# A perceiver block on one core: the first rooms of the way up, the transposes ahead of it, and two operations of its last units are placed differently

## The chip, the cores and the metric

The kernel runs on one core of a Trainium2 chip. The metric is the time of one execution on the device in microseconds (us). Times of single instructions come from one execution recorded by the hardware profiler.

The core has a matrix engine, TensorE (PE in the profile; its weight loads are PEld), and VectorE (DVE), ScalarE (ACT) and GpSimd (POOL) for work on tiles. SyncE (SP) issues most of the transfers; SPq, ACTq and POOLq are the queues for them. Matmul results go to banks of the accumulator memory (PSUM), from where DVE and ACT take them.

## The reference

There are 32 sequences of 64 tokens with 512 features. Three stages each add to x:

```
x = x + xattn(layernorm(x), ctx, mask)          # attention over 256 context rows
x = x + attn(layernorm(x), wq, wkv, wo, ...)    # 16 heads, causal, low rank
x = x + ffn(layernorm(x), gate, up, down, expert, gamma, beta)

def ffn(t):
    logits = t @ gate                            # 8 gates
    scale  = sum of the two largest logits
    h = square(relu(t @ up))                     # 512 -> 2048
    y = h @ down + (t @ expert) * scale          # 2048 -> 512
    return layernorm(y) * gamma + beta
```

## The kernel before, in words

Every float32 operand is split into a high part, which ACT copies (`split`, L147), and a low part, the rest, which DVE subtracts (L149). A product is then three matmuls: high by high, low by high, high by low (`mm3`, L174 on). The large products are tiled 2 by 2 and each tile of the four needs seven products instead of eight (`SEVEN`); GpSimd makes the sums that this needs (`sums`, L155), and `combine` (L158 to L169) puts the seven results together: a copy by ACT (L160), then DVE's L162, L163, L165, L166 and L168. Each of these frees a bank that PE wants for the unit after next.

The stages by time in the profile: projections and the context attention to about 240 us, the attention to about 550, **the way out** (product with wo, L718 to L726) to about 758, **the way up** (L1144 on) from 773 to 931, **the way down** from 931 to 1086, then the last layer norm.

The way out goes through units (block of 256 tokens, slot k of 8). Beside its units the code places other work by unit number: `TURN_AT` transposes a finished block (`o_t`), `MULT_AT` multiplies it by the expert (`o_expert`), `UP_READ` and `UP_PUT` read slots of the up weights and split them (`put_slot`, four instructions: two copies on ACT, two subtractions on DVE). After the last unit come the transposes of the last block (L985 on), three of the four parts of its split features (`right`, xr0_0 to xr0_2; copies at L1067, subtractions at L1065), and the last `o_expert` (cpe14, cpe15, L179 to L181), whose output tile `mo` is stored by ACT's queue (L1023). Then the way up begins.

The way up has four passes (b = 0 to 3) of eight units (n = 0 to 7, slots in the order 0, 1, 5, 6, 7, 2, 3, 4). A unit is 42 matmuls of 256 columns (`up_seven`, L1156), its four banks come from one of two pools in turn (`ps_f[n % 2]`), its combination ends in a tile `uo`, ACT applies relu and square (L1226, L1227), and the result goes to memory as `hd`. In a pass the next pass's features are split (xr1_0 to xr1_3, and so on). In the first pass the remaining up slots are split, one in each unit; in the last pass the down slots are split (`put_slot(..., "down")`) and the first pairs of the way down are read back and split (`read_home`, L698; `left`, which gives the tiles `hl`). `read_home` reads into a tile that is there from the start; `left(u, pins=...)` is the split of unit u.

`settle(n, ...)` issues n transposes of a 128 by 128 tile into a bank whose content isn't used. It stands ahead of the way up (n = 8) and at units 5 and 32 of the way down (n = 4).

The order on each engine is made by the framework's scheduler out of the order of the program, its own cost estimates, and the tiles' rooms: a new tile in a room waits for the last reader of the old one. `with after(ins)` (the `pins` of `split`, `right`, `put_slot` and `left`) sets an operation no earlier in the order than `ins`; without it the scheduler may place the operation as far ahead as its inputs allow. Each engine then works its list in that order.

Two rooms matter for the change: `mo0` is allocated ahead of the way out (L1070), and the last `o_expert` uses a later tile of the same pool, `ap`; that pool closes ahead of the way up, and the tiles of the pool `fp` (`uo`, `up1`) take over its space.

Of the kernel before, what the change touches and what calls it, by code (L numbers as in the profile page):

```python
# [18 lines left out]
P = 128  # L19
# [36 lines left out]
MULT_AT = (21, 25, 31, 39, 47, 55, 63)  # L56

FEATURES_AT = (2, 4)
UP_READ, UP_PUT = (1, 2, 5, 6, 7), (3, 5)

BETA_AT = 60

# [24 lines left out]
def perceiver_block(ctx: ExitStack, tc: tile.TileContext, x, mem, mask, wq_a, bq_a, qnw, wq_b, bq_b,  # L87
# [87 lines left out]
    def mm3(ps, pairs):  # L175

        n = len(pairs)
        for j, (ah, al, bh, bl) in enumerate(pairs):
            nc.tensor.matmul(ps, ah, bh, start=(j == 0), stop=False)  # L179
            nc.tensor.matmul(ps, al, bh, start=False, stop=False)  # L180
            nc.tensor.matmul(ps, ah, bl, start=False, stop=(j == n - 1))  # L181


    with ExitStack() as mla:
# [816 lines left out]

    def o_expert(blk, xh, xl, _):

        mo = mos.pop(blk, None) or ap.tile([P, 2, D], FP, tag="mo", name=f"mo{blk}")
        for tt in range(2):
            i = 2 * blk + tt
            sl = slice(tt * P, (tt + 1) * P)
            pes = []
            for c in (slice(256, NE), slice(0, 256)):
                pe = ps_t.tile([P, D], FP, tag="T", name=f"cpe{i}_{c.start}")  # L1010
                mm3(pe[:, 0 : c.stop - c.start], [
                    (xh[:, k, sl], xl[:, k, sl], wes[0][:, k, c], wes[1][:, k, c]) for k in range(NKD)
                ])
                pes.append(pe)
            t8 = sp.tile([P, 8], FP, tag="t8", name=f"t8{i}")
            nc.vector.max(t8, pes[0][:, 256:264])
            gs = sp.tile([P, 1], FP, tag="gs", name=f"gs{i}")
            nc.vector.tensor_tensor(gs, t8[:, 0:1], t8[:, 1:2], ALU.add)
            if tt:
                yield  # L1020
            nc.scalar.mul(mo[:, tt, 256:512], pes[0][:, 0:256], gs)
            nc.scalar.mul(mo[:, tt, 0:256], pes[1][:, 0:256], gs)
        nc.scalar.dma_start(mo_d[blk], mo)  # L1023
        yield

    xr, xc, xw = {}, {}, []

    def read_x(b, kk, room=None, behind=None):

# [37 lines left out]
                    ins = nc.scalar.copy(t[:, to], src)  # L1067
        return ins

    mos = {0: ap.tile([P, 2, D], FP, tag="mo", name="mo0")}  # L1070
    put_slot(ORDER[2], "wo")
    xt, xns, xT, x2s, dones, read = {}, {}, {}, {}, {}, 5
    for u, (blk, k) in enumerate(out_units):
# [61 lines left out]
    xT = o_t(NB - 1, xns.pop(NB - 1), lambda: next(scaled))  # L1135
    for part in range(3):
        right(0, part, (dones[NB - 1][0], xT[2][1]))
    put_slot(ORDER[2], "up", pins=xT[2])
    for _ in o_expert(NB - 1, *xT):
        pass  # L1140
    pc.close()


# [2 lines left out]
    with ExitStack() as pu:  # L1146
# [3 lines left out]
        def up_seven(ps, k, b, n, steps):  # L1150
            wh, wl = (t[:, 0:7].rearrange("p a (k f) -> p a k f", k=2) for t in wts[k])

            def product(s, parts, first=False, last=False):
                i, j = SEVEN[s]
                for m, (kk, w, low) in enumerate(parts):
                    nc.tensor.matmul(  # L1156
                        ps[s // 2][:, s % 2], w[:, i, kk], xr[b, 2 * kk + low][:, j],
                        start=(first and m == 0), stop=(last and m == len(parts) - 1),
                    )

            most = [(0, wh, 0), (0, wl, 0), (0, wh, 1), (1, wh, 0), (1, wl, 0)]
            rest = [(1, wh, 1)]
            one, two = (0, 2, 4, 6), (1, 3, 5)
            late = None
            if n == 0:
                with after(settle(8, ps, wh[:, 0, 0], ident2, None) if b == 0 else None):
                    for s in one:
                        product(s, most, first=True)
            if n == 7:
                for s in one:  # L1170
                    product(s, rest, first=True)
                for s in (0, 2, 4):
                    product(s, most, last=True)
                for s in two:
                    product(s, rest, first=True)
                if b + 1 < NB // 2:
                    late = right(b + 1, 3)
            for s in range(7):
                if n == 0 and s in one:
                    product(s, rest, last=True)  # L1180
                elif n < 7:
                    product(s, most + rest, True, True)
                elif s in two or s == 6:
                    product(s, most, last=True)
                if s in (1, 3, 5, 6):
                    with after(late if s == 3 else None):
                        next(steps)
# [8 lines left out]
                nc.sync.dma_start(h_d[b][:, k, 3:7], w)  # L1196

        stores = []
        right(0, 3)
        behind = read_slot(ORDER[5], "up", behind=reads[-1])  # L1200
        for b in range(NB // 2):
            if b == NB // 2 - 1:
                first = [(blk, k) for ks in (ORDER[:5], ORDER[5:]) for blk in DOWN[:2] for k in ks]
                out_units[:] = first + [(blk, k) for blk in DOWN[2:] for k in ORDER]
            for n, k in enumerate(ORDER):
                m = n - 3 if b == 0 else n - 1
                summed = None
                if 0 < b < NB // 2 - 1 and m in (0, 1):
                    read_x(b + 1, m)
                if b == 0 and n in (1, 2):  # L1210
                    behind = read_x(1, n - 1, x_room(1, n - 1), behind)
                if b == 0 and n in (0, 1):
                    behind = read_slot(ORDER[n + 6], "up", behind=behind)
                if b == NB // 2 - 1 and 0 < n < 7:
                    read_slot(ORDER[n - 1], "down")
                if b == NB // 2 - 1 and n == 4:
                    read_home(2, from_h, None)
                if b == NB // 2 - 1 and n in (5, 6):
                    read_pair(n - 2, from_h)
                ps = banks(ps_f[n % 2], f"up{b}_{k}")  # L1220
                o = fp.tile([P, 5, TB], FP, tag="o", name=f"uo{b}_{k}")
                p1 = fp.tile([P, TB], FP, tag="p1", bufs=2, name=f"up1_{b}_{k}")
                done = []
                up_seven(ps, k, b, n, combine(p1, ps, o, done))
                for q in (slice(0, 2), slice(2, 4)):
                    nc.scalar.activation(o[:, q], o[:, q], AF.Relu)  # L1226
                    act = nc.scalar.activation(o[:, q], o[:, q], AF.Square)  # L1227
                pins = (act, done[-1])
                o4 = o[:, 0:4].rearrange("p (c t) (a n) -> p c t a n", c=2, a=2)
                w = None  # L1230
                if not bare(b, k):
                    w = ccp.tile([P, 8, P], FP, tag="c", name=f"uw{b}_{k}").rearrange("p (d t) n -> p d t n", t=2)
                    at = [o4[:, i, :, a] for i in range(2) for a in range(2)] + [w[:, d] for d in range(4)]
                    summed = sums(at, LEFT)
                if b == 0 and n < 5:
                    put_slot(ORDER[n + 3], "up", pins=pins)
                if b == NB // 2 - 1 and 1 < n < 7:
                    put_slot(ORDER[n - 2], "down", pins=pins)
                if b == NB // 2 - 1 and n == 2:
                    for u in range(2):  # L1240
                        read_home(u, from_h, None)
                if b == NB // 2 - 1 and n == 3:
                    left(0, pins=(done[0], done[-1]))
                if b == NB // 2 - 1 and n == 5:
                    left(1, pins=(done[0], done[-1]))
                if b == NB // 2 - 1 and n == 6:
                    left(2, pins=(done[0], done[-1]))
                if b == NB // 2 - 1 and n == 7:
                    read_pair(5, from_h)
                if stores and (b, n) != (NB // 2 - 1, 7):  # L1250
                    store_h(*stores.pop(0))
                stores.append((b, k, o4, w))
                if b + 1 < NB // 2:
                    if m in (0, 1):
                        sum_x(b + 1, m, summed)
                    for q in (PARTS_FIRST if b == 0 else PARTS).get(m, ()):
                        right(b + 1, q, pins)

    with ExitStack() as pd:
# [82 lines left out]
        for u, (blk, k) in enumerate(out_units):  # L1342
            if k == ORDER[0]:
                pss[blk] = banks(ps_f[DOWN.index(blk) % 2], f"dp{blk}")
            while read <= min(max(u + READ_AHEAD, 2 * u + 1), u + READ_FAR, last_unit):
                read_pair(read, from_h, room_for(read))
                read += 1
            for v in [v for v in bares if v <= u + SUM_AHEAD]:
                c = bares.pop(v)
                with after(pows[-1]):  # L1350
# [15 lines left out]
                store_h(*stores.pop(0))  # L1366
            if u == 6:
                nc.sync.dma_start(gab, gamma.partition_broadcast(P))
            if u in (4, 6, 8):
                put_slot(ORDER[3 + u // 2], "down")  # L1370
            if u in (2, 4):
                read_slot(ORDER[5 + u // 2], "down")
            outs = [d for d in outs if step(d, low)]
# [52 lines left out]
```

## Time and profile before

| what | before |
|---|---|
| median of three timed runs | 1103.37 us (1101.33 to 1103.40) |
| the profiled execution | 1098.9 us |
| its span | 1096.7 us |
| its granted TensorE clock, mean | 0.998 |
| PE busy | 97% of the span |
| DVE, ACT, POOL busy | 70%, 50%, 46% |
| matmuls | 10201 |
| PE waits: op L725 for DVE hl L149 | 3.7 us in 4 |
| PE waits: ops L985 for DVE on L139 | 1.0 us in 1 |
| PE waits: up L1156 for DVE uo L168 | 0.6 us in 1 |

How to read it: a line of a view names an engine, a line of the code, the operation and its tiles, out<-in. The timeline's rows start with the start and the duration in us; in brackets stands the idle time of the engine just before, and after "<-" what ended it. Matmuls are pipelined: a record lasts about 0.28 us while the next one starts after about 0.115, so rows overlap. A row of the view by stretch gives, for each engine, the time that it was busy and in brackets its instructions, then the granted clock, the share of the DMA engines and GB/s.

### The profile page before, as it was taken

The page shows a single profiled execution, that of the slowest core. Times are in us where ns is not written, and L with a number is a line of the kernel's source. Part 1 is how long each engine was busy: PE and PEld are TensorE (multiplying, and loading weights), DVE is VectorE, ACT ScalarE, POOL GpSimd, SP SyncE. Part 2 cuts the span into 40 slices and gives each one's busy share as a digit, 9 for nine tenths or more (in the row PEclk, how much of TensorE's full clock was granted, in tenths as well). Part 3 has the DMA queues.
Part 4 walks back from the last instruction along what each step waited for, and adds up shares of the span by engine and source line. Part 5 has one row for each costly group of instructions (what it writes and reads, how often), then busy time and mean ns, then how long its engine had stood idle before and what let it go on. Part 6 is the DMA issues. An engine that isn't in the chain of part 4 may idle for free.

```text
span 1096.7 us, 26072 instructions
## 1 busy us (share of the span) xinstructions
PE 1066.9 (97%) x10201; PEld 983.6 (90%) x10201; DVE 769.0 (70%) x1369; ACT 546.1 (50%) x1051; POOL 508.1 (46%) x691
## 2 busy tenths in 40 slices
PE   8999999999999999999998999999999999999996
PEld 6667777679999999999988999999999999999996
DVE  5666666657666666656787866667785658898786
ACT  4444444533433444434475544445676567755553
POOL 2333333326788778874570000003238970065671
PEclk9999999999999999999999999999999999999999
DMA  8867666343776778655487776779646689998672
GB/s 259 263 216 231 206 212 203 124 161 121 260 234 245 260 247 294 249 207 195 160 324 276 263 241 213 231 235 359 218 156 202 221 247 366 310 309 257 206 232 79
DMA packets 195386, 254.67 MB, mean 232 GB/s; under 512 B 18544, under 2 KB 140032, under 8 KB 195264
## 3 DMA queue, kind: packets, MB, share of 16 engines
q1 hardware_dynamic: 190704, 240.92, 67.0%
q10 hardware_dynamic: 3456, 8.39, 2.2%
q0 software_dynamic: 1104, 3.70, 0.9%
q8 instruction: 80, 1.31, 0.5%
q14 instruction: 42, 0.34, 0.1%
HBM read 146.67 MB, written 106.30 MB: 231 GB/s over the span
## 4 chain that ended last, share of the span: by engine, by line
PE 59%; DMA 10%; POOL 9%; DVE 8%; issue 7%; ACT 5%; SPq 1%; DVEq 0%; POOLq 0%; ACTq 0%
PE up L1156 9%; PE pss L773 5%; PE psq L179 4%; PE psq L180 4%; PE psq L181 4%; PE op L725 3%; PE op L726 3%; PE op L723 3%; PE psv L817 3%; DMA hd<-uo 2%; PE pse L179 2%; PE pse L181 2%; PE pse L180 2%; DMA x1d<-xt 2%; DMA vd<-vw 2%
## 5 line engine op out<-in xcount | busy, mean ns | idle before, releaser
L755 DVE SCALAR_TENSOR_TENSOR qe<-pse,bqp,cq 64x256 f32<-64x256 f32 x256 | 123.7, 483 | 76.5 <-PE pse L181 70.7
L1156 PE MATMUL up<-xr,wh_up 128*128 128x256 f32 x896 | 157.6, 280 | 0.6 <-DVE uo L168 0.6
L1156 PEld LDWEIGHTS up<-xr,wh_up 128*128 128x128 f32 x896 | 137.5, 189 | 1.0 <-issue 0.7
L725 PE MATMUL op<-wh_wo,hl 128*128 128x256 f32 x448 | 124.4, 279 | 3.7 <-DVE hl L149 3.7
L723 PE MATMUL op<-wh_wo,hl 128*128 128x256 f32 x448 | 124.0, 280 | 0.6 <-ACT hl L147 0.6
L725 PE MATMUL dp<-wh_down,hl 128*128 128x256 f32 x448 | 124.5, 278 | 0.0
L723 PE MATMUL dp<-wh_down,hl 128*128 128x256 f32 x448 | 124.4, 278 | 0.0
L726 PE MATMUL dp<-wl_down,hl 128*128 128x256 f32 x448 | 124.3, 277 | 0.0
L149 DVE TENSOR_TENSOR hl<-c,hl 128x896 fp32r<-128x896 f32 x84 | 94.3, 1126 | 42.3 <-ACT hl L147 42.0
L1156 PE MATMUL up<-xr,wl_up 128*128 128x256 f32 x448 | 123.7, 280 | 0.0
L726 PE MATMUL op<-wl_wo,hl 128*128 128x256 f32 x448 | 123.5, 277 | 0.0
L147 ACT CAST hl<-c 128x896 fp32r<-128x896 f32 x84 | 79.0, 942 | 77.7 <-PE op L726 38.0
L179 PE MATMUL psq<-qa_hi,qh 128*128 128x256 f32 x384 | 112.5, 293 | 0.0
L180 PE MATMUL psq<-qa_hi,ql 128*128 128x256 f32 x384 | 106.4, 277 | 0.0
L181 PE MATMUL psq<-qa_lo,qh 128*128 128x256 f32 x384 | 106.2, 276 | 0.0
L725 PEld LDWEIGHTS op<-wh_wo,hl 128*128 128x128 f32 x448 | 84.3, 188 | 4.8 <-DVE hl L149 4.7
L723 PEld LDWEIGHTS op<-wh_wo,hl 128*128 128x128 f32 x448 | 83.6, 188 | 1.5 <-ACT hl L147 0.8
L723 PEld LDWEIGHTS dp<-wh_down,hl 128*128 128x128 f32 x448 | 84.6, 189 | 0.0
L725 PEld LDWEIGHTS dp<-wh_down,hl 128*128 128x128 f32 x448 | 84.1, 188 | 0.4 <-DVE hl L149 0.4
L1156 PEld LDWEIGHTS up<-xr,wl_up 128*128 128x128 f32 x448 | 84.2, 188 | 0.0
L726 PEld LDWEIGHTS op<-wl_wo,hl 128*128 128x128 f32 x448 | 84.1, 188 | 0.0
L726 PEld LDWEIGHTS dp<-wl_down,hl 128*128 128x128 f32 x448 | 84.1, 188 | 0.0
(233 smaller groups left out, 3146.6 us busy)
## 6 DMA issues: line engine op xcount, KB each, us to landing
c<-vd SPq DMA_DIRECT2D x58, 448.0 KB, 4.2
cx<-in_ctx SPq DMA_DIRECT2D x32, 512.0 KB, 4.6
vd<-vw SPq DMA_DIRECT2D x29, 512.0 KB, 3.6
hd<-uo SPq DMA_DIRECT2D x107, 128.0 KB, 3.3
hd<-uw SPq DMA_DIRECT2D x21, 512.0 KB, 3.3
dcw<-hd SPq DMA_DIRECT2D x18, 448.0 KB, 5.6
vd<-v SPq DMA_DIRECT2D x30, 256.0 KB, 3.5
wd_wo<-pw_wo SPq DMA_DIRECT2D x8, 896.0 KB, 4.9
```

The costliest lines, as they stand in the source:

```text
L147: copy = nc.scalar.copy(hi, src)
L149: return copy, engine.tensor_tensor(lo, src, hi.bitcast(FP), ALU.subtract)
L179: nc.tensor.matmul(ps, ah, bh, start=(j == 0), stop=False)
L180: nc.tensor.matmul(ps, al, bh, start=False, stop=False)
L181: nc.tensor.matmul(ps, ah, bl, start=False, stop=(j == n - 1))
L723: first = nc.tensor.matmul(ps[s // 2][:, s % 2], h[:, a], wh[:, b], start=(k == 0 and s % 2 == 0), stop=False)
L725: nc.tensor.matmul(ps[s // 2][:, s % 2], l[:, a], wh[:, b], start=False, stop=False)
L726: ins = nc.tensor.matmul(ps[s // 2][:, s % 2], h[:, a], wl[:, b], start=False, stop=last)
L755: rope = nc.vector.scalar_tensor_tensor(qe[64 * a : 64 * a + 64, :], pe[r, :], bqp[r, p : p + 1], cq[r, a, :], ALU.add, ALU.mult,)
L773: nc.tensor.matmul(ps[64 * j : 64 * j + 64, pj, b, :], qs[2 * pj + j][a][:, sl], kT[:, a, kt], start=(a == 0), stop=(a == 1),)
L817: nc.tensor.matmul(o, kv[a, i, :], t[a, bp, :], start=True, stop=True)
L1156: nc.tensor.matmul(ps[s // 2][:, s % 2], w[:, i, kk], xr[b, 2 * kk + low][:, j], start=(first and m == 0), stop=(last and m == len(parts) ...
```

## The change

It has four parts. First, `UP_PUT` loses its second unit: the up slot `ORDER[1]` is no longer split at the fifth unit of the last block but just ahead of the last `o_expert`, pinned behind the last unit's split and the low part of the last transposes. The slot `ORDER[2]`, which stood there, goes to the start of the way up, its low part pinned behind `right(0, 3)`. Second, `mo0` is no longer allocated ahead; each `o_expert` takes its own tile. So the first rooms of the way up lie elsewhere. Third, `mm3` returns its last matmul, and the settling transposes ahead of the way up become four, pinned behind the last one of the expert. Fourth, in the last pass the slot `ORDER[4]` for the way down and the split `left(2)` leave unit 6: the slot goes to unit 1 and `left(2)` to unit 0 of the way down's loop, both without pins.

```diff
-UP_READ, UP_PUT = (1, 2, 5, 6, 7), (3, 5)
+UP_READ, UP_PUT = (1, 2, 5, 6, 7), (3,)
...
-            nc.tensor.matmul(ps, ah, bl, start=False, stop=(j == n - 1))
+            ins = nc.tensor.matmul(ps, ah, bl, start=False, stop=(j == n - 1))
+        return ins
...
-        mo = mos.pop(blk, None) or ap.tile([P, 2, D], FP, tag="mo", name=f"mo{blk}")
+        mo = ap.tile([P, 2, D], FP, tag="mo", name=f"mo{blk}")
...
-                mm3(pe[:, 0 : c.stop - c.start], [
+                made.append(mm3(pe[:, 0 : c.stop - c.start], [
                     (xh[:, k, sl], xl[:, k, sl], wes[0][:, k, c], wes[1][:, k, c]) for k in range(NKD)
-                ])
+                ]))
...
-    mos = {0: ap.tile([P, 2, D], FP, tag="mo", name="mo0")}
     put_slot(ORDER[2], "wo")
...
-    put_slot(ORDER[2], "up", pins=xT[2])
+    put_slot(ORDER[1], "up", pins=(low[0], xT[2][1]))
     for _ in o_expert(NB - 1, *xT):
         pass
+    ends = made[-1]
...
-                with after(settle(8, ps, wh[:, 0, 0], ident2, None) if b == 0 else None):
+                with after(settle(4, ps, wh[:, 0, 0], ident2, ends) if b == 0 else None):
...
-        right(0, 3)
+        put_slot(ORDER[2], "up", pins=(xT[2][0], right(0, 3)))
...
-                if b == NB // 2 - 1 and 1 < n < 7:
+                if b == NB // 2 - 1 and 1 < n < 6:
                     put_slot(ORDER[n - 2], "down", pins=pins)
...
-                if b == NB // 2 - 1 and n == 6:
-                    left(2, pins=(done[0], done[-1]))
...
+            if u == 0:
+                left(2)
...
-            if u in (4, 6, 8):
-                put_slot(ORDER[3 + u // 2], "down")
+            if u in (1, 4, 6, 8):
+                put_slot(ORDER[max(4, 3 + u // 2)], "down")
```

In the order of the instructions that results, up to 755 us nothing is moved. From there: the settling transposes stand four together ahead of the way up, where before one stood there and seven among the matmuls of the last expert; in the first pass, L168 of each combination stands ahead of the splits, where it stood behind them; the two low halves of xr1_3 stand ahead of the combination of `uo0_3`, where they stood behind it; the ACT copy of `left(2)` stands ahead of the relu of `uo3_0`, where it stood behind the copy L160 of `up1_3_3`; and half of a `wl_down` split stands between L162 and L163 of `uo3_3`. The order on SP and on POOL's queue is nearly the same.

More of the change, by code (lines that the diff above doesn't have):

```diff
@@ L1024, in o_expert @@
         yield
-    xr, xc, xw = {}, {}, []
+    xr, xc, xw, made = {}, {}, [], []
     def read_x(b, kk, room=None, behind=None):
```

## The prediction

> **What bounds the kernel now.** I read the busy shares first, then the waits, then counts of matmuls by stretch, then the rows of the three small engines around the places that the change touches.
>
> ```profile
> span 1096.7 us, 26072 instructions
> PE 1066.9 (97%) x10201; PEld 983.6 (90%) x10201; DVE 769.0 (70%) x1369; ACT 546.1 (50%) x1051; POOL 508.1 (46%) x691
> L1156 PE MATMUL up<-xr,wh_up 128*128 128x256 f32 x896 | 157.6, 280 | 0.6 <-DVE uo L168 0.6
> ```
>
> TensorE (PE) is busy for 97% of the span. The group of the way up (L1156) shows 0.6 us of idle time in 896 matmuls. So two things alone can move the end: a pause of PE, and the spacing of its matmuls. The change removes no matmul; work that it moves on VectorE (DVE), ScalarE (ACT) or a queue counts only through PE's pauses.
>
> The spacing isn't one number. In the view of busy time by stretch, the third value is PE's time and the (x) its matmuls:
>
> ```profile
> 773.00:793.00 20.00, 20.00 (x172) 20.00 (x171) 14.02 (x23) 11.88 (x23) 5.83 (x8) 1.00 0.54 183
> 810.00:830.00 20.00, 20.00 (x179) 20.00 (x178) 13.40 (x25) 12.99 (x26) 16.37 (x21) 1.00 0.71 233
> 860.00:880.00 20.00, 20.00 (x172) 20.00 (x171) 12.09 (x21) 10.96 (x20) 18.12 (x23) 1.00 0.66 220
> 950.00:970.00 20.00, 20.00 (x179) 20.00 (x178) 15.31 (x17) 11.07 (x16) 10.33 (x14) 1.00 1.14 316
> ```
>
> All four are full of matmuls of one shape, PE is never idle, the granted clock is 1.00, and yet 172 or 179 matmuls fit. A record lasts 0.28 us and both ends count, so the spacing is 20.28/172 = 117.9 ns or 20.28/179 = 113.3 ns: 4.5 ns, or 4%, apart. Followed along the trace, the spacing keeps its value for long stretches and changes after a pause (fast after the one at 808.0, slow again after two of 0.1 us at 847), or at the four "settle" transposes in the way down (slow to fast at 943.5 and 1065.5, two of two). The way up begins slow at 773.07, is fast for 330 of its 1344 matmuls (809 to 847), and slow for the other 1014.
>
> **The change, part by part.** The sum is made against the profiled execution's 1098.9 us (span 1096.7 and 2.2 around it), 4.5 below the median of 1103.4; the difference found is then put on the median.
>
> *1. Settling transposes.* Before, one of the eight stands directly ahead of the way up, and seven lie among the last expert's matmuls. After, all four that are left stand together behind the last of them. Four in a row take 943.41 to 944.09, 0.67 us, where two matmuls take 0.24: 0.44 for four, 0.11 for one. **+0.33 us.** What it buys is term 6.
>
> *2. Handover from the way out.* One slot's split leaves unit 61, where DVE holds it ahead of the last combination:
>
> ```profile
> 755.37 2.63 DVE L149 TENSOR_TENSOR wl_up<-wl_up,wh_up 128x1024 fp32r<-128x1024 f32 x2
> 757.92 0.68 DVE L162 TENSOR_TENSOR oo<-op,op 128x512 f32<-128x512 f32 x1
> 764.13 1.00 DVE L139 TENSOR_SCALAR on<-oo,lnmv_o,rs_o 128x512 f32<-128x512 f32 x2 [0.74 <-POOL rs_o L127]
> ```
>
> L162 could start at 757.05, when the products of its bank are done, 0.87 earlier. The MAX8 of the expert (L1016) then stands ready no sooner than 759.55, which eats part: the chain to L139 and the transposes comes 0.65 us earlier. PE idles 1.02 us there ("PE ops L985 <- DVE on L139"), so all of it is gained. **−0.65**, between 0 and −1.02. The split itself (2.6 us of DVE, 1.8 of ACT) moves to 769–776 beside the last expert and the first up unit, where DVE next idles 4.67 us (to 780.10); the first rooms no longer wait for the store of the expert's output, so that the first combination starts some 2.7 us earlier and the extra split fits.
>
> *3. The stall at 808.*
>
> ```profile
> 803.28 0.68 DVE L166 TENSOR_TENSOR uo<-up,up 128x512 f32<-128x512 f32 x1
> 804.29 2.10 DVE L149 TENSOR_TENSOR wl_up<-wl_up,wh_up 128x1024 fp32r<-128x1024 f32 x2 [0.32 <-ACT wh_up L147]
> 806.30 0.96 DVE L1065 TENSOR_TENSOR xr<-xp,xr 128x768 fp32r<-128x768 f32 x1
> 807.17 1.23 DVE L1065 TENSOR_TENSOR xr<-xc,xr 128x1024 fp32r<-128x1024 f32 x1
> 808.30 0.42 DVE L168 TENSOR_TENSOR uo<-uo,up 128x256 f32<-128x256 f32 x1
> 808.63 0.69 DVE L162 TENSOR_TENSOR uo<-up,up 128x512 f32<-128x512 f32 x1
> ```
>
> The last step of a combination (L168), which frees PE's bank, stands behind a split and two halves of xr. PE restarts at 808.87, 0.57 us idle and 0.7 lost. In the changed order L168 stands ahead of them. **−0.7**, between 0 and −0.7.
>
> *4. First unit of the second pass (b=1).* The same reordering puts the two halves of xr1_3 ahead of the combination of the unit before last (uo0_3). In the rows of before they come after it (811.39 and 812.44, behind L162 at 808.63). They wait for ACT's copies of 0.83 and 1.04 us (809.96, 810.68), and these stand behind four relu/square instructions (0.63 each); then DVE needs 0.96 + 1.23 and L162, 0.69. So the bank comes free at about 813.4, and PE asks for it at 810.7 (fast since 773) to 811.9 (slow): a pause of 1.5 to 2.7. The low end stays 0, since the operands may be ready earlier than I reckon. **+2.0.**
>
> *5. Third pair and the first down unit.* `left(2)` loses its pins. Its ACT copy then stands in the last pass's first unit, behind the copy L160 of uo3_0 and ahead of uo3_0's relu and square; before it stood at 928.50. It waits for a transfer, seen in the view of the tile hl and of SP's queue:
>
> ```profile
> 895.55 2.38 SPq L698 DMA_DIRECT2D hl<-hd  x3
> 895.62 0.35 ACT L160 COPY up<-up 128x256 f32<-128x256 f32 x1
> 898.15 0.37 ACT L160 COPY up<-up 128x256 f32<-128x256 f32 x1 [2.17 <-PE up L1156]
> 928.50 0.95 ACT L147 CAST hl<-hl 128x896 fp32r<-128x896 f32 x1
> 930.36 0.42 DVE L163 TENSOR_TENSOR up<-uo,up 128x256 f32<-128x256 f32 x1
> DMA to landing us min/median/max: 4.6/5.7/7.4
> ```
>
> The third of these reads is issued at 897.1 and takes the 7.4: it lands at 904.5. Until then ACT holds back two relus, two squares and the next unit's L160, done at 898.15 before. After: 904.5 + 0.94 (copy) + 2.2 (four activations) + 0.35 (L160) + 0.65 (L162) + 0.42 (L163) = 909.0, when the bank of the unit after next is free; PE wants it at 906.7. Pause: 0 (if the read lands 2.4 us earlier) to 2.4. I take **+1.0**: the read shares the queue with five stores, so its landing is the least certain number here.
>
> Near the end of the pass DVE is full (18.70 of 20 us between 912 and 932), so lost time isn't made up. The bank of the first down matmul is freed by the last L163 above, at 930.78, 0.65 before it is wanted at 931.4 (after slow spacing). After, ACT and DVE are some 4 us late there, less the pause of 2.4 that PE has made itself, and half a wl_down split (1.22) stands between L162 and L163: 4.0 + 1.2 − 2.4 − 0.65 = 2.1. If the first pause doesn't come, 1.22 − 0.65 = 0.6 is left. At most 3.2, where slots delay it too. **+2.0.** The slot split taken out of the last pass doesn't help here: it has no pins either, and its instructions still stand ahead of the last two combinations on DVE. If the hl2 copy were held back, this term would be 0.6.
>
> The strict order of ACT is what makes this a price. [...]
>
> *6. Spacing.* If four transposes ahead of the way up act as they did twice in the way down, the first pass runs fast up to the pause of term 4: 300 × 4.5 ns = **−1.3**. After a pause the spacing has gone either way, so behind 811 I take it as before: 0. The ends: fast to 943, 1014 × 4.5 ns and 110 more in the way down, −5.0; slow throughout, +1.5.
>
> [...]
>
> **Sum.** 0.33 − 0.65 − 0.7 + 2.0 + 1.0 + 2.0 − 1.3 = **+2.7 us**: 1101.6 for an execution like the profiled one, 1106.1 on the median.
>
> **Rivals.**
>
> *A, faster.* The spacing is fast from 773 to the way down (−5.0), and pauses 4 and 5 come out at their low ends (0, 0, 0.6): 0.33 − 0.65 − 0.7 − 5.0 + 0.6 = −5.4, 1098.0. For it: two of two settlings. Against it: the fast stretch before ended in a pause of 0.1 us, and the order of ACT shows the block. It decides if the hl read lands before 902; partial forms reach to −2.2.
>
> *B, no difference.* Term 5's block is short, since a faster pass reads and stores earlier: 0.33 − 0.65 − 0.7 + 1.5 + 0 + 0.6 − 1.3 = −0.2, 1103.2.
>
> *C, the transposes do nothing.* Of eight before, four stood together among the expert's matmuls and the spacing stayed slow. Then term 6 is 0 to +1.5, and with the stalls at 2.7, 2.0 and 2.0 the sum is 0.33 − 0.65 − 0.7 + 6.7 + 0 to 1.5 = +5.7 to +7.2: up to 1110.6.
>
> **How the numbers follow.** A measurement of this kernel tells 0.2%, 2.2 us, from no change. The forecast and its neighbours between +2.2 and +4.5: 0.32; C and beyond: 0.24; B: 0.25; A and its partial forms: 0.19. So slower 0.56, same 0.25, faster 0.19. The predicted time is the forecast's, 1106. The range goes from A's partial forms, 1100, to C's end, 1111; about 2 in 10 are left out. The forecast's own range is 1105.6 to 1108.
>
> **What would show it.** Right: the first up stretch with 179 matmuls in 20 us; PE idle about 0.4 us ahead of the last transposes; no pause near 808 and one of 1.5 to 2.7 at the first unit of b=1, released by DVE L162; an ACT copy of hl with a wait for DMA near 896–904; a pause of PE near 907 and one at its first L723 of the way down. Wrong: no ACT wait there, or PE's idle time in the way up still under 1 us, or 172 matmuls in each stretch of the first pass. If the idle time is as predicted and the end is not, the spacing is the step that failed.

## The result, and the profile after

| | before | after |
|---|---|---|
| median of 14 runs on the same chips, us | 1101.26 (1097.47 to 1106.72) | 1109.72 (1104.45 to 1114.85) |
| ratio, 95% interval | 1 | 1.0067 (1.0045 to 1.0089) |
| the profiled execution, its span, us | 1098.9, 1096.7 | 1109.17, 1107.3 |
| first up matmul to first down matmul, us | 158.1 | 165.8 |
| from there to the end of the span, us | 165.5 | 165.5 |

The kernel became slower by 0.67%, 7.4 us of 1101.26. (The medians themselves lie 8.5 us apart; the ratio, which agrees with that of the two means, is used throughout.) Of the 10.6 us between the two profiled spans, 3.0 are there before the first up matmul (773.07 and 776.03). They are hardly an effect of the change: 1.6 come before the way out begins, and 1.8 in the way out, where the order is still the same but PE waited 2.84 us ahead of 591.59 (2.05 in before) and then had clock 0.50 for 3.4 us; 0.4 are gained from there to the first up matmul. The other 7.7 lie between the first up and the first down matmul (773.07 to 931.16, 776.03 to 941.80). The rest of the way down takes the same time. I use the length of this stretch to compare profiles below, since it leaves out the differences of the earlier stages.

The waits of PE in this stretch of the changed kernel, from the view of waits (us in total, times, longest); before had one line there, 0.6 us for DVE uo L168:

```profile
PE up L1157 <- DVE up L163: 3.1, 1, 3.1
PE up L1157 <- DVE uo L162: 2.9, 1, 2.9
PE dp L724 <- DVE up L163: 0.3, 1, 0.3
```

Both large pauses are those of the prediction's terms 4 and 5. The first, on DVE and PE of the changed kernel (start, duration, line, operation, and in brackets the idle time before):

```profile
814.20 1.05 DVE L1066 TENSOR_TENSOR xr<-xp,xr 128x768 fp32r<-128x768 f32 x1 [1.14 <-PE up L1157]
815.18 1.74 DVE L1066 TENSOR_TENSOR xr<-xc,xr 128x1024 fp32r<-128x1024 f32 x1
816.84 1.27 DVE L162 TENSOR_TENSOR uo<-up,up 128x512 f32<-128x512 f32 x2
817.66 0.36 PE L1157 MATMUL up<-xr,wh_up 128*128 128x256 f32 x1 [2.90 <-DVE uo L162]
```

xr1_3's two halves, the first of which waits itself, stand ahead of L162, and L162 ends PE's pause. The second, on ACT, DVE and PE:

```profile
900.92 0.35 ACT L160 COPY up<-up 128x256 f32<-128x256 f32 x1
910.37 0.94 ACT L147 CAST hl<-hl 128x896 fp32r<-128x896 f32 x1 [9.10 <-DMA hl<-hd]
911.21 1.15 ACT L1227 ACTIVATE uo<-uo 128x512 f32<-128x512 f32 x2
912.27 1.13 ACT L1228 ACTIVATE uo<-uo 128x512 f32<-128x512 f32 x2
913.30 0.62 ACT L160 COPY up<-up 128x256 f32<-128x256 f32 x2
913.74 0.69 DVE L162 TENSOR_TENSOR uo<-up,up 128x512 f32<-128x512 f32 x1 [1.31 <-POOL uw L155]
914.46 0.42 DVE L163 TENSOR_TENSOR up<-uo,up 128x256 f32<-128x256 f32 x1
915.03 0.36 PE L1157 MATMUL up<-xr,wh_up 128*128 128x256 f32 x1 [3.14 <-DVE up L163]
```

ACT stands still for 9.10 us ahead of one copy whose data are not there, and four activations and two copies L160 stand behind it. (POOL is named ahead of DVE's L162, but DVE's row starts in the middle of ACT's L160 row, of which it needs the first of two.)

What the prediction didn't have stands behind that pause. In the view by stretch, the ninth value is PE's granted clock (PE, PEld, DVE, ACT, POOL come first, each with its count):

```profile
911.60:915.00 3.40, 0.28 (x3) 0.08 (x2) 2.06 (x4) 2.33 (x6) 1.97 (x3) 1.00 0.52 174
916.00:917.00 1.00, 1.00 (x6) 1.00 (x6) 0.97 (x3) 1.00 (x3) 0.00 (x0) 0.50 0.21 82
917.00:918.00 1.00, 1.00 (x7) 1.00 (x6) 1.00 (x3) 1.00 (x3) 0.36 (x1) 0.50 1.05 377
920.00:925.00 5.00, 5.00 (x45) 5.00 (x44) 3.59 (x6) 3.56 (x6) 0.69 (x1) 1.00 1.02 341
```

PE is busy again, but at clock 0.50 until 919.0: 17 matmuls start up to 214 ns apart instead of 118, which costs another 1.6 us together with the restart.

The spacing, in the same view: fast at first, as predicted (before had 172 in its first 20 us), then slow, where before had 179 between 810 and 830:

```profile
780.00:800.00 20.00, 20.00 (x179) 20.00 (x178) 16.68 (x27) 14.39 (x25) 5.38 (x7) 1.00 0.42 123
820.00:840.00 20.00, 20.00 (x173) 20.00 (x172) 9.25 (x21) 13.49 (x26) 17.30 (x25) 1.00 0.71 232
```

### The profile page after: what moved, and what is told of

It reads as the page before. It is cut to its first block, busy times and chain, and to the rows that moved or that the text cites. A ratio compares the mean times of both kernels' runs of the same rounds, so it can differ in the third digit from the quotient of the medians.

```text
span 1107.3 us, 26065 instructions
## 1 busy us (share of the span) xinstructions
PE 1070.8 (97%) x10197; PEld 987.5 (89%) x10197; DVE 768.9 (69%) x1369; ACT 544.9 (49%) x1051; POOL 506.8 (46%) x691
```

## The experiments

The table has every kernel's ratio to the kernel before on its chip (95% interval), the stretch from the first up to the first down matmul in its profile, and PE's pauses of over 1 us in it with what ended them. Twelve runs of each were compared with before, but 9 of the sixth and 6 of the seventh. One profile is one execution; the ratio decides what a kernel is worth, the profile shows where it is lost. The execution that was profiled for xr_pin was the slowest of its nine (1117.63 us, median 1108.21).

| kernel | ratio | stretch, us | pauses over 1 us |
|---|---|---|---|
| before | 1 | 158.1 | none |
| changed | 1.0067 (1.0045 to 1.0089) | 165.8 | 2.90 (L162), 3.14 (L163) |
| left_only | 1.0036 (1.0019 to 1.0053) | 159.8 | 4.17 (L163) |
| slots_only | 1.0023 (1.0004 to 1.0041) | 161.7 | 1.00 (L163), 2.92 (L162), 1.59 at the first down matmul |
| settle_only | 0.9989 (0.9967 to 1.0012) | 156.3 | 1.85 at the first down matmul |
| both | 0.9998 (0.9978 to 1.0019) | 158.7 | 1.27 (L162), 1.59 at the first down matmul |
| left_back | 1.0015 (0.9996 to 1.0033) | 160.8 | 2.91 (L162), 1.04 at the first down matmul |
| xr_pin | 1.0065 (1.0040 to 1.0091) | 165.3 | 1.40 (L162), 3.56 (L163), 1.06 at the first down matmul |
| fill | 1.0085 (1.0058 to 1.0112) | 169.0 | 2.54, 3.20 (both L162), 2.83 (L168) |
| late_each | 1.0019 (0.9998 to 1.0040) | 159.6 | 2.76 (L168) |
| rest_only | 0.9994 (0.9975 to 1.0013) | 156.1 | 1.87 at the first down matmul |
| last_units | 1.0004 (0.9986 to 1.0022) | 161.2 | 2.33 (L168) |
| last_spread | 0.9998 (0.9981 to 1.0015) | 156.4 | 1.86 (L168) |
| room_spread | 0.9978 (0.9954 to 1.0001) | 158.4 | none |

The theory at the start: two instructions that stand at another place, xr1_3 on DVE and the hl copy on ACT, make two pauses, and these are the loss. The rival: the loss lies in the spacing of the matmuls, and the pauses are absorbed.

**1. left_only: the kernel before with `left(2)` moved, and nothing else.**

```diff
-                if b == NB // 2 - 1 and n == 6:
-                    left(2, pins=(done[0], done[-1]))
...
+            if u == 0:
+                left(2)
```

> The kernel before with only `left(2)` moved to the way down's loop without pins. Theory (two pauses made by two reordered instructions): ACT's copy of hl stands idle over 5 us for its DMA near 901 to 910, PE pauses 2 to 4 us for DVE L163 near 907 to 915, and if that pause is over 3 us the granted clock drops after it as in the changed kernel (1.6 us more); the time is 2 to 6 us above before. Rival (the loss lies in the matmuls' spacing, and the pauses are absorbed later): no more than 1 us above before.

Measured: 1.0036, 4.0 us of the median of before there (1103.17). The pause is there, longer than in the changed kernel; the views of ACT's and PE's waits:

```profile
ACT hl L147 <- DMA hl<-hd: 9.3, 1, 9.3
```

```profile
PE up L1156 <- DVE up L163: 4.2, 1, 4.2
```

Behind it 16 matmuls run at clock 0.50. The stretch grew by only 1.7 us, not by 4.2 + 1.5, since the spacing in this execution was fast for nearly all of it: from 778.7 to 907 it shows 113 ns, without the change of the transposes. So the theory holds for the pause, and the spacing is a second thing that varies by itself.

**2. slots_only: the kernel before with the up slots moved.**

```diff
-UP_READ, UP_PUT = (1, 2, 5, 6, 7), (3, 5)
+UP_READ, UP_PUT = (1, 2, 5, 6, 7), (3,)
-    put_slot(ORDER[2], "up", pins=xT[2])
+    put_slot(ORDER[1], "up", pins=(low[0], xT[2][1]))
-        right(0, 3)
+        put_slot(ORDER[2], "up", pins=(xT[2][0], right(0, 3)))
```

> The kernel before with only the slots of the way up moved (UP_PUT and the two put_slot lines). Theory: the 0.57 us idle time at 808 goes, PE pauses 2 to 3.5 us for DVE L162 in the first unit of b=1, since xr1_3 stands ahead of uo0_3's combination; the way down's first unit and b=3 are as before; time 1 to 3 us above before. Rival (spacing): pause under 1 us, time within 1 us of before.

Measured: 1.0023, 2.5 us. PE's waits in the stretch:

```profile
PE up L1156 <- DVE uo L162: 2.9, 1, 2.9
PE dp L723 <- DVE up L163: 1.6, 1, 1.6
PE up L1156 <- DVE up L163: 1.0, 1, 1.0
```

The pause at b=1 is made by this part alone. It has two others: 1.0 us near 804, where DVE holds an additional split and the bank comes late, and 1.6 at the first down matmul, where before had none. That the way down's first unit stays as before, as I expected, is wrong.

**3. settle_only: the kernel before with the four pinned transposes.**

```diff
+        return ins
...
-                with after(settle(8, ps, wh[:, 0, 0], ident2, None) if b == 0 else None):
+                with after(settle(4, ps, wh[:, 0, 0], ident2, ends) if b == 0 else None):
```

> The kernel before with only the settling transposes changed: four, pinned behind the expert's last matmul. Theory: some 177 to 179 matmuls in 773 to 793 where before had 172 (spacing 113 ns), so the first pass ends 1.0 to 1.5 us earlier, less 0.3 for three more transposes there; what the spacing is behind the pause at 808 is open, so the time is 2 us below to 1 us above before. Rival (the transposes do nothing): 172 in that stretch and 0 to 0.5 us above.

Measured: 0.9989 (0.9967 to 1.0012), no difference that can be told. In the profile the way up is fast almost throughout:

```profile
778.00:798.00 20.00, 20.00 (x179) 20.00 (x178) 15.07 (x25) 13.07 (x22) 6.45 (x8) 1.00 0.52 166
```

Last up matmul less first: 154.2 us against 158.0. But the first down matmul then waits 1.85 us, where the kernel before didn't wait, and the clock falls behind that pause too (17 matmuls, 1.6 us), so nearly all of the 3.8 us are given back. DVE's release of that bank had 0.65 us in hand at the slow spacing; a PE that arrives 3.8 us earlier uses that up.

**4. both: the changed kernel with `left(2)` back in unit 6 and xr1_3 pinned.**

```diff
-                    late = right(b + 1, 3)
+                    late = right(b + 1, 3, (None, low6))
...
                 pins = (act, done[-1])
+                low6 = done[-1]
...
+                if b == NB // 2 - 1 and n == 6:
+                    left(2, pins=(done[0], done[-1]))
...
-            if u == 0:
-                left(2)
```

> The changed kernel with two edits: `left(2)` back in unit 6 of the last pass with its pins, and the low part xr1_3 pinned behind uo0_3's last combination step. Theory: both pauses (2.9 and 3.1 us idle) and the drop of the clock behind the second (1.6 us) go, the 0.57 us at 808 stays gone; 6 to 9 us below the changed kernel, between 3 us below and 1 us above before. Rival (spacing): the spacing stays slow from 814 on, at most 3 us below the changed kernel.

Measured: 0.9998. Against the changed kernel's 1.0067 that is 0.69%, 7.6 us: the whole loss is gone with these two placements, and the rival (at most 3 us) falls. What is left of the pauses:

```profile
PE dp L724 <- DVE up L163: 1.6, 1, 1.6
PE up L1157 <- DVE uo L162: 1.3, 1, 1.3
```

**5. left_back: of the two, only `left(2)` put back.** The edit is the second half of the diff above.

> The changed kernel with `left(2)` back in unit 6 of the last pass with its pins. Theory (the block of ACT and the slower clock behind it): no wait of ACT's hl copy, no pause near 907 to 915, granted clock 1.00 throughout; the pause at the first unit of b=1 stays near 2.9 us; the first down matmul waits 1 to 2 us, since DVE is late by its splits; 3 to 5 us below the changed kernel, 1.5 to 4 us above before. Rival (the pause only moves to the way down): within 1.5 us of the changed kernel.

Measured: 1.0015, 5.7 us below the changed kernel by the two ratios. The pause in b=3 is gone (0.2 us is left of it); the one at b=1 stays at 2.91 and the first down matmul waits 1.04, as expected. The clock didn't stay at 1.00 as expected: in this execution it fell behind the pause of 2.91 (17 matmuls, 1.6 us), where the changed kernel's pause of 2.90 had no such effect; the last section shows how the two differ.

**6. xr_pin: of the two, only xr1_3 pinned.** The edit is the first half.

> The changed kernel with the low half xr1_3 pinned behind uo0_3's last combination step. Theory: the pause of 2.9 us at the first unit of b=1 falls to 1 to 1.5 us (what is left is xr1_3 itself, that PE needs at that unit's second part), the pause of 3 to 4 us in b=3 stays; 1 to 2.5 us below the changed kernel. Rival (PE is only earlier for the pause in b=3, which grows by as much): within 0.7 us of the changed kernel, the b=3 pause longer.

Measured: 1.0065, no gain at all against 1.0067. Here the rival was right:

```profile
PE up L1157 <- DVE up L163: 3.6, 1, 3.6
PE up L1157 <- DVE uo L162: 1.4, 1, 1.4
PE dp L724 <- DVE up L163: 1.1, 1, 1.1
```

The pause at b=1 fell by 1.5 us, and the pause in b=3 and the wait of the first down matmul grew by 0.4 and 0.8. As long as the later block stands, curing the earlier pause gives nothing that these runs can tell. With the block gone (left_back to both) the pin is worth 0.17% by the ratios, which is inside their intervals.

**7. fill: 20 transposes ahead of the matmul that waits in b=3.**

```diff
+            if (b, n) == (3, 3):
+                filled = settle(20, before_ps[-1], wh[:, 0, 0], ident2, lasts[-1])
```

> The changed kernel with 20 more transposes of the settling kind, into the half bank that no product uses, between the unit before the pause in b=3 and the matmul that waits. The pause's end is set by ACT and DVE, so they fill about 2.2 us of it. Theory (the granted clock drops for about 3.5 us because PE idles for over 3 us): idle time of about 1 us there and the clock stays at 1.00; 1 to 2 us below the changed kernel. Rival (transposes don't count as work for the clock): the clock still falls to 0.5 behind the pause and the time is within 0.5 us of the changed kernel.

Measured: 1.0085, no faster than the changed kernel. The test failed as a test: the half bank belongs to the unit before, and the first transpose waited for that unit's combination:

```profile
913.73 0.38 PE L1157 MATMUL up<-xr,wh_up 128*128 128x256 f32 x1 [3.20 <-DVE uo L162]
917.76 1.54 PE L714 MATMUL up<-ident,wh_up 128*128 128x128 f32 x6 [2.83 <-DVE uo L168]
```

So it added a second pause instead of filling the first, and what it was to tell, whether transposes keep the clock up, stays open.

**8. late_each: `both`, with two down slots later and four transposes ahead of each pass.**

```diff
-                if b == NB // 2 - 1 and 1 < n < 6:
-                    put_slot(ORDER[n - 2], "down", pins=pins)
+                if b == NB // 2 - 1 and n in (2, 3, 4, 6):
+                    put_slot(ORDER[min(n - 2, 3)], "down", pins=pins)
...
-                put_slot(ORDER[max(4, 3 + u // 2)], "down")
+                put_slot(ORDER[max(4, 3 + u // 2)], "down", pins=low if u == 1 else (None, None))
...
-                with after(settle(4, ps, wh[:, 0, 0], ident2, ends) if b == 0 else None):
+                with after(settle(4, ps, wh[:, 0, 0], ident2, lasts[-1] if lasts else ends)):
```

> The changed kernel with `left(2)` back and pinned, xr1_3 pinned, the last pass's split of ORDER[3] one unit later (behind uo3_3's combination), ORDER[4]'s pinned behind the way down's unit 1, and four settling transposes ahead of each of the four passes. Theory: the spacing is 113 ns through most of the way up (177 to 179 matmuls in 20 us), the first down matmul waits under 0.7 us, since the split that stood ahead of its bank's release is behind it; 0.5 to 4 us below before. Rival (a faster PE only meets ACT and DVE earlier): pauses elsewhere take it back, within 1 us of before.

Measured: 1.0019. The wait at the first down matmul went (0.11 us start to start, no idle time), and the spacing was fast from 820 on to the end of the pass. But the transposes of the second pass write into the bank that the combination's last step frees, so PE waited 2.76 us there for L168, where `both` had waited 1.27 for L162. My edit made that pause.

**9. rest_only: what remains of the change without slots, `left(2)` and transposes.** The room of the expert's output, and ORDER[4] in the way down.

```diff
-    mos = {0: ap.tile([P, 2, D], FP, tag="mo", name="mo0")}
...
-                if b == NB // 2 - 1 and 1 < n < 7:
+                if b == NB // 2 - 1 and 1 < n < 6:
...
-            if u in (4, 6, 8):
-                put_slot(ORDER[3 + u // 2], "down")
+            if u in (1, 4, 6, 8):
+                put_slot(ORDER[max(4, 3 + u // 2)], "down")
```

> The changed kernel with `left(2)`, the up slots and the settling transposes as before: what is left is the expert's output tile without the early allocation and the slot ORDER[4] moved to the way down without pins. Theory (the loss is all in the up slots and in `left(2)`): within 1.5 us of before, no pause over 1.5 us between 773 and 931. Rival (the new rooms or the unpinned slot cost 2 us by themselves, since the single parts measured so far add up to 5.3 of the 7.4 us): 1.5 to 3 us above before.

Measured: 0.9994, the theory's side, except that a pause of 1.87 us stands just at the stretch's end, at the first down matmul. The room does what it says: the first combination starts 4.8 us behind the first up matmul (778.60, 773.82), before 7.0. And there is no pause at 808, though L168 still stands behind the split and xr's halves, and though the spacing is fast (179 in 778 to 798): DVE gets to L168 at 807.50, in time. So the pause at 808 came from the late first combination as much as from the order.

**10 and 11. last_units and last_spread: the kernel before with the four transposes, the last down slots later, and, in the second, the pairs earlier.** The down slots as in 8; the pairs in last_spread:

```diff
-                if b == NB // 2 - 1 and n == 3:
-                    left(0, pins=(done[0], done[-1]))
-                if b == NB // 2 - 1 and n == 5:
-                    left(1, pins=(done[0], done[-1]))
-                if b == NB // 2 - 1 and n == 6:
-                    left(2, pins=(done[0], done[-1]))
+                if b == NB // 2 - 1 and n in (2, 3, 5):
+                    left((2, 3, 5).index(n), pins=(done[0], done[-1]))
```

> The kernel before with the four settling transposes and the last pass's two last down slots later (ORDER[3] behind uo3_3's combination, ORDER[4] in the way down's unit 1 behind that unit's pair, both pinned). Theory (what the faster spacing gains is given back at the first down matmul, because DVE does splits ahead of that bank's release): that wait, 1.8 us with the settling transposes alone, falls under 0.5 us; 1 to 4 us below before. Rival (the wait moves on to the slots or pairs of the way down's units 1 to 8): within 1.2 us of the kernel with the settling transposes alone.

> The same with the three pairs split one unit earlier each (behind the combinations of units 2, 3 and 5, after their reads have landed). Theory: no pause at the first down matmul and none from pairs, 1.5 to 4.5 us below before. Rival (an earlier pair is a copy that waits for its DMA, as `left(2)` in the changed kernel): ACT waits for hl's DMA over 1 us and PE pauses near 905 to 915, no better than before.

Measured: 1.0004 and 0.9998; neither gains, where 1 to 4.5 us were expected. The wait at the first down matmul is gone in both. In its place stand pauses of 2.33 and 1.86 us at 808, since the spacing of the first pass was fast and the first combination still waits for the expert's store (DVE stands idle for 5.43 and 4.97 us ahead of it); and in last_spread there are three short ones at 939 to 941 for wl_down and wh_down, since the slot ORDER[4] now comes too late, with clock 0.50 behind them. Pinned behind a combination, an earlier pair didn't wait for its DMA: last_spread shows no such wait of ACT between 890 and 925, where left_only had 9.3 us.

**12. room_spread: before with transposes, the room, the pairs spread and ORDER[4] one unit earlier than in 11.**

> The kernel before with the four settling transposes, the expert's output tile without the early allocation, the pairs split behind units 2, 3 and 5 of the last pass, ORDER[3] behind uo3_3's combination and ORDER[4] pinned in the way down's unit 0: the parts of the change that showed no loss, and the cures for the waits that were left. Theory (with DVE earlier by the store it no longer waits for, the pause near 808, 1.9 us in the kernel with the three pairs spread, goes, and the first down matmul doesn't wait): the way up takes 155 to 157 us, no pause over 0.7 us in it; 1 to 4 us below before. Rival (the gain is smaller than the spread of runs, or comes back as waits of the way down for its slots): within 1 us of before.

Measured: 0.9978 (0.9954 to 1.0001), the lowest of all, 2.4 us of 1104.66, with an interval that just reaches 1. PE doesn't pause once between 770 and 959. In the profile the stretch takes 158.4 us and not 155 to 157, because the spacing turned slow after 20 fast matmuls:

```profile
780.00:800.00 20.00, 20.00 (x171) 20.00 (x171) 16.04 (x27) 15.13 (x26) 3.92 (x6) 1.00 0.39 111
```

## Why the prediction was right, and where it was not

The side was right, the time lay in the range, and the size of the loss was off: +2.7 forecast, +7.4 measured, and 1109.7 us lies outside the forecast's own 1105.6 to 1108. Order and releasers of the pauses came as worked out; their sizes did not, and the errors partly cancelled, which was luck: the second part of term 5 was 1.6 us too large, and the slower clock, 1.6 us, was not in the sum at all. By the terms, those from 3 on measured against the 7.7 us between the first up and the first down matmul:

- *Terms 1 and 2* (+0.33, −0.65): from the last way-out matmul to the first up matmul it took 15.30 us before and 14.88 after, −0.42 against −0.32.
- *Term 3* (−0.7): right, the pause at 808 is gone; one of 0.12 us, up to 804.97, stands in its place. L168's new place isn't the only cure: rest_only has the old order and no pause there.
- *Term 4* (+2.0, between 0 and 2.7): 2.90 idle. Mechanism and releaser right, size just outside my bounds.
- *Term 5, first part* (+1.0, between 0 and 2.4): this is the step that failed in size. The pause was 3.14, and the clock behind it cost 1.6 more, together some 4.9 with the restart. The working gave 2.4 with the landing of before, and 0.6 more for the later landing makes 3.0; I took a low value because the landing might come earlier, and it came later. The order of ACT that makes this a price shows in the changed kernel's rows: 9.10 us idle ahead of the copy, and the first activation behind it only at 911.21. The slowest of the three reads took 8.0 us (7.4 before) and landed at 910.34; by the view of the tile hl, lines of the wait and of the landing:

```profile
  ACT hl L147: 9.1, 1
  DVE hl L149: 7.6, 1
DMA to landing us min/median/max: 4.7/5.8/8.0
```

- *Term 5, second part* (+2.0): 0.27 idle, 0.44 lost. The sum didn't hold together here: this part subtracts a first pause of 2.4, while the first part goes in at 1.0. It was right that this wait depends on the first pause; the longer that one is, the more DVE and ACT catch up. Where the first pause is gone (left_back, both) it is 1.0 to 1.6. The length of the first pause isn't all, though: in xr_pin it is 3.56 and this wait 1.06.
- *Term 6* (−1.3): the first pass was fast, for some 330 matmuls, but before had 330 fast ones behind its pause at 808, and in the changed kernel these are slow. I kept them "as before"; together the spacing gave 0. It also rested on too little: with the four pinned transposes all ten profiles begin fast, but three of them fall back after 20 to 25 matmuls, and of four profiles without them two (left_only, rest_only) are fast nearly from the start too.

So, each as the lateness of the next matmul's start: 3.07 (term 4) + 3.31 + 1.6 (term 5's pause and clock) + 0.44 + 0.29 (first down matmul, 805) − 0.74 − 0.27 (808 and two small ones of before) = 7.7.

The rivals: A and B fell, since the pauses came. C's mechanism fell (the first pass did turn fast), though its pauses, 6.7 together (3.07 + 3.31 + 0.44 measured), and its sum of +5.7 to 7.2 are near what was measured. The order of the instructions on the engines told the pauses and the releasers; none of the rows of before could show the clock's price, since its only long pause on the path (2.05 us at 590) left the clock at 1.00.

By the ratios the single parts give +3.6 (left), +2.3 (slots), −1.1 (settling) and −0.6 (rest) in thousandths, 4.2 together where the whole gives 6.7. The difference is of the size of the intervals, and whether the parts make each other worse stays open.

## What to carry to other kernels

An unpinned operation that waits for a transfer is not free because its engine has room: here ACT worked its list in order, stood idle for 9.10 us ahead of one copy, and four activations and two copies behind it waited as well. So look up where the scheduler put it, and pin it behind work that ends after the transfer has landed. When a pause of the bounding engine is cured, ask which deadline comes next: here a faster PE met DVE's splits at the first down matmul, and curing the earlier of two pauses gave nothing while the later one stood. Price a pause of PE of 2 to 3 us with the slower clock that may follow it, some 1.6 us here, not by its length alone.

## What the runs showed of the hardware

*The clock behind a pause.* Taking the pauses of PE in the way up and at the first down matmul, as single ones without another close by: of 1.6 us and less none was followed by clock 0.50; of 1.85, 1.86, 2.33, 2.76, 2.91 and 2.92 each was, of 1.87, 2.54 and 2.90 none, six times out of nine between 1.85 and 2.92; of 3.14, 3.56 and 4.17 all three. The slow stretch was mostly 16 or 17 matmuls at 213 ns, about 3.5 us, and cost 1.5 to 1.6 us whatever the pause's length (once 12 matmuls, once 14). In last_spread a pause of 1.86 us did it:

```profile
810.00:811.00 1.00, 1.00 (x6) 1.00 (x6) 0.52 (x2) 1.00 (x2) 0.92 (x2) 0.50 0.49 136
811.00:812.00 1.00, 1.00 (x7) 1.00 (x6) 0.00 (x1) 1.00 (x3) 0.89 (x2) 0.50 0.52 142
```

The clock records of the traces show more. In the changed kernel the clock is 0.50 from 7.65, 591.33 and 915.60 us, each time for 3.413 us, and these starts lie 171 and 95 times 3.413 us apart; in before its two changes (6.00 and 1091.44) lie 318 such steps apart, and in left_only the slow stretches begin at 588.93, 759.59 and 913.19, 50 and 45 steps apart. In the other profiles, too, the changes lie whole steps apart; by the views of six of them a slow stretch takes 3.4 us. In these runs the slower clock went with how much of a pause fell into one step. Here are two pauses of one length by these steps, 2.90 in the changed kernel (first two rows) and 2.91 in left_back:

```profile
813.20:816.61 3.41, 1.56 (x14) 1.36 (x12) 2.41 (x2) 2.45 (x5) 3.25 (x4) 1.00 0.41 115
816.61:820.03 3.42, 2.37 (x20) 2.40 (x21) 3.42 (x9) 0.62 (x2) 0.89 (x1) 1.00 0.49 159
818.62:822.03 3.41, 1.23 (x11) 1.26 (x12) 3.41 (x6) 0.16 (x1) 1.94 (x2) 1.00 0.27 96
822.03:825.44 3.41, 3.41 (x19) 3.41 (x18) 2.40 (x6) 2.90 (x6) 1.15 (x2) 0.50 0.86 266
```

The steps cut the first into 1.85 and 1.05 us without a matmul, and the clock stays; 2.18 us of the second lie in one step, and the next step is slow. Over all profiles, without their first 20 and last 13 us, a step with 1.95 us or more without a matmul, by PE's records with their modelled ends, was followed by clock 0.50 in 14 of 14 cases, one with 1.69 to 1.86 in 8 of 11, and one with less only once (1.32 us, the three short pauses of last_spread). Among them are 2.58 and 2.84 us (changed kernel) and 2.18 (left_back), all followed by it; 1.85 (settle_only) and 1.86 (last_spread), followed by it; and 1.85 (changed kernel) and 1.71 (before), not followed by it. So in these runs most of the chance was where the pause fell: the 1.87 of rest_only were cut into 0.69 and 1.18.

*Two spacings at one clock.* Matmuls of one shape ran 113 or 118 ns apart at granted clock 1.00 (179, or 171 to 173, in 20 us). What sets it I could not settle. Four transposes directly ahead of the way up were followed by the fast one in ten of ten profiles, but not for long in three; a pause changed it either way (before has 172 in 20 us ahead of the one at 808 and 179 behind it, the changed kernel 179 ahead of the one at 817 and 173 behind it); and in left_only and rest_only it came without either. The stretch without its last pause is up to 4 us shorter in the profiles where it is fast throughout (154.0 from the first to the last up matmul in rest_only, 158.0 in before), and this may be a part of why single runs of one kernel differ by 10 us (1104.45 to 1114.85 in the changed kernel).
